# Layer pair on one core: residuals laid into PSUM by ScalarE, sums added by DMAs, and the seven-product form from group 4

## The chip, the core and the metric

The kernel runs on one core of a Trainium2 chip. The engines of the core work side by side, each on its own queue of instructions: TensorE (PE in the profile, its weight loads PEld), VectorE (DVE), ScalarE (ACT), GpSimd (POOL) and SyncE (SP), which issues most DMAs. The metric is the device time of one execution in microseconds (us), lower is better; times are medians over runs.

## The reference

The input is 2 images of 56 x 56 tokens with 384 channels in float32. Layer 0 is a neighbourhood attention with an MLP, layer 1 a mixer with an MLP:

```python
# layer 0
h = neighborhood_attention(layer_norm(x, ln1_g, ln1_b), w_qkv, ...)   # 12 heads, 7 x 7 window
x = x + h
y = layer_norm(x, ln2_g, ln2_b)
x = x + (gelu(y @ w1 + b1) @ w2 + b2)                                  # 384 -> 1536 -> 384
# layer 1
h = layernorm(x, n1_g, n1_b)
p = h @ w_in + b_in                                                    # 384 -> 768
local = depthwise_conv_3x3(p, k_conv)
lr, rl = ema_scan(local, axis=2), ema_scan(local, axis=2, reverse=True)  # along a line
tb, bt = ema_scan(local, axis=1), ema_scan(local, axis=1, reverse=True)  # along a column
mixed = 0.25 * (lr + rl + tb + bt) + local                             # y[i] = 0.6 y[i-1] + 0.4 x[i]
mixed = layernorm(mixed, on_g, on_b)
x = x + (mixed @ w_out + b_out)
h2 = layernorm(x, n2_g, n2_b)
x = x + (gelu(h2 @ w1 + b1) @ w2 + b2)
```

The change touches the MLP of layer 0 and all of layer 1; the attention stays as it is.

## The kernel before

The 6272 tokens are 49 tiles of 128. After the attention, the rest of the kernel (`passes`) goes over them twice, in groups of 4 tiles (512 tokens).

The *first pass* (loop at L1712, groups 0 to 12, of which group 0 has one tile) computes the MLP of layer 0 for group g and `project_in` (L1472, the product with `w_in`) for group g-1. `hidden` (L1190) makes one of twelve 128-channel slices of the hidden layer: three matmuls of 512 columns and a GELU on ScalarE. `tokens` (L1198) multiplies the hidden layer by `w2` for one tile of 128 tokens, twelve matmuls of 384 columns into one of two PSUM banks, `y` and `y_end`, which `bank()` gives out in turn. L1846 then adds the residual `x` on VectorE and writes `x2`, and `norm.add` takes the statistics of that row. `store_x2` writes `x2` to DRAM.

In groups 1 and 2 (`EARLY`), in the hidden layer of group 3, and in the tail below, products take a *seven-product form* (`hidden_by_seven` L1538, `tokens_by_seven` L1620): two-by-two blocks are multiplied with seven products instead of eight, from sums of weights (`sums_of_w1` L1509, `sums_of_w2` L1601), of the input (`sums_of_input` L1523) and of the hidden layer, which GpSimd makes.

The convolution and the scans of layer 1 are VectorE work that runs *beside* TensorE, in a pool opened by `begin_convolution` (L1713). `Band` (L1237) handles some lines of one image for one of six 128-channel slices (`BANDS`: four bands for image 0, three for image 1). It loads `pt` from DRAM, ScalarE takes the centre tap (`centre`), VectorE the other eight taps (L1281), `loc` is stored; then both scan directions along the lines (`both_ways` L1225, in parts of at most `LINES` = 20 lines) give `both`, L1297 forms `both*share + loc`, and this goes to `mix_d` in DRAM. `Columns` (L1306) does the scans along columns of one slice of one image: `turn` transposes the lines (GpSimd for the first job of an image, else ScalarE, L1328), `both_ways` scans in quarters of 14 lines, L1355 adds `share` times that to `mixed`, loaded from `mix_d`, and the sum is stored back.

`Beside` (L112) sets where this work stands in the program's order. It holds a list of jobs; each job is a generator that issues an instruction or two and yields its estimated us (`us`, L1221). After each piece of TensorE work the program calls `beside.go(worth)`: worth times `rate` is added to a balance, and jobs are stepped until it is used up. `MLP, PRO, ROW = 2.25, 2.5, 6.2` are the worths of a hidden slice, a `project_in` slice and a token row in the first pass, `MLP_D, OUT_D, ROW_D` those of the second stage; the rate is 0.9 and becomes 1.0 once image 1 is reached. `until(name)` issues all that is left up to a job, and `later` puts off a store by a step.

The *second stage* (loop at L1885, groups 0 to 5) takes the MLP of layer 1 for group g and `project_out` (L1434) for group g+1: twelve matmuls with `w_out` a row, `xc = ps*rs + x` on VectorE (L1440), and the statistics of that. The statistics of `mixed` come from `measure_beside` (L1423), which has TensorE turn `mx` into a PSUM tile (`xi`). `load_mix` (L1373) loads `mx` and `x`. For the group where both images meet, `half_way` = 6, it first issues all that is left of the convolution.

The *tail* (loop at L1926) does groups 6 to 11 in the seven-product form, with the statistics turned by VectorE (`measure_by_vector` L1405) and the transposes by VectorE (`turned` L1162); group 12 has one tile. Its pool and the weight sums come at the start of group 5 of the second stage (L1886).

Rows of biases (`b2_0`, `b_out`, `b2_1`) are added by `add_row` (L1122) to whole groups of 4 tiles ahead of their use as residuals. `Norm` (L205) holds a group's statistics: `close` takes the root on GpSimd, `shift` (VectorE) the product of mean and root, `apply_by_scalar` normalises on ScalarE.

Of the kernel before, what the change touches and what calls it, by code (L numbers as in the profile page):

```python
# [33 lines left out]
F32 = mybir.dt.float32  # L34
# [29 lines left out]
    ((0, 19), (19, 37), (37, 47), (47, 56)),  # L64
    ((0, 18), (18, 36), (36, 56)),
)
HALF = H // 2
LINES = 20
# [46 lines left out]
class Beside:  # L115
# [3 lines left out]
    def __init__(self):  # L119
        self.jobs, self.due, self.finished, self.idle = [], 0.0, set(), True  # L120
        self.late, self.rate = [], 0.9
        self.steps = self.run()
# [8 lines left out]
    def later(self, issue):  # L131

        self.late.append([1, issue])

    def step(self):
        got = next(self.steps)
        for entry in self.late:
            entry[0] -= 1
        while self.late and (self.late[0][0] < 0 or got is None):
            self.late.pop(0)[1]()  # L140
        return got
# [17 lines left out]
    def go(self, worth):  # L159
        self.due += self.rate * worth  # L160
# [15 lines left out]
def block_kernel(ctx: ExitStack, tc: tile.TileContext, ins: dict, out: bass.AP):  # L176
# [25 lines left out]

# [3 lines left out]
    class Norm:  # L206
# [15 lines left out]
        def close(self, k, n=P, first=0):  # L222
# [4 lines left out]
            nc.gpsimd.tensor_tensor(rs, rs, mhalf[:n, first:k], ALU.pow)  # L227

# [853 lines left out]
    def passes(xs, xn, w1, w2, between=lambda ps: None):  # L1082
# [9 lines left out]
        half_way = next(g for g, (t, n) in enumerate(dgroups) if t + n * P > T1)  # L1092
# [29 lines left out]
        def add_row(x, n, name):  # L1122

            engine = nc.vector if beside.busy() else nc.gpsimd
            engine.tensor_tensor(
                x[:, :n, :], x[:, :n, :], row(name).unsqueeze(1).to_broadcast([P, n, C]), ALU.add
            )

        def prepare_w_out():
# [11 lines left out]
            t = flat(half("sums", "out", 3))  # L1141
            nc.vector.tensor_copy(t[:2, 2 * C : 3 * C], ps[:2, :])
# [56 lines left out]
        def tokens(lhs, w, k, ps=None):  # L1199

            ps = bank() if ps is None else ps
            for m, t in enumerate(lhs):
                nc.tensor.matmul(  # L1203
                    ps, lhsT=t[:, k * P : (k + 1) * P], rhs=w[:, m, :],
                    start=m == 0, stop=m == len(lhs) - 1,
                )
            return ps

# [28 lines left out]
        class Band:  # L1237
# [21 lines left out]
            def centre(self):  # L1259
                if self.loc is None:  # L1260
                    self.loc = half("loc", "work")
# [6 lines left out]
            def steps(self):  # L1268
# [5 lines left out]
                for dy in (-1, 0, 1):  # L1274
# [13 lines left out]
                beside.later(lambda: nc.sync.dma_start(  # L1288
                    out=loc_d[self.b][self.m, :, at], in_=flat(loc)))
                both = half("both", "out", 3)[:, : self.n]  # L1290
                parts = -(-self.n // LINES)
                for i in range(parts):
                    part = slice(self.n * i // parts, self.n * (i + 1) // parts)
                    yield from both_ways(both[:, part], loc[:, part])
                    if i == 0:
                        behind = beside.behind()
                nc.vector.scalar_tensor_tensor(  # L1297
                    flat(both), flat(both), share, flat(loc), ALU.mult, ALU.add
                )
                if isinstance(behind, Band):  # L1300
                    behind.centre()
                yield us(self.n)
                beside.later(lambda: nc.sync.dma_start(
                    out=mix_d[self.b][self.m, :, at], in_=flat(both)))

        class Columns:  # L1306
# [16 lines left out]
            def turn(self, copy):  # L1323
                c, t = len(self.lines), half("line", "work")
# [9 lines left out]
            def steps(self):  # L1334
# [5 lines left out]
                for c in range(2):  # L1340
                    t = self.lines[c]
                    for i in range(0, HALF, QUARTER):
                        yield from both_ways(t[:, i : i + QUARTER], t[:, i : i + QUARTER])
                        if c == 0 and i == 0:
                            self.turn(nc.scalar.copy)
                            for h in range(2):
                                mixed.append(half("mixed", "out", 3))
                                nc.sync.dma_start(out=flat(mixed[h]), in_=self.rows(mix_d, h))
                    if c == 1:
                        behind = beside.behind()  # L1350
                    for i in range(0, HALF, QUARTER):
                        at = slice(c * HALF + i, c * HALF + i + QUARTER)
                        for h in range(2):
                            to = mixed[h][:, :, at]
# [707 lines left out]
```

## Time and profile before

| | us |
|---|---|
| median of 3 runs (lowest, highest) | 2594.55 (2593.26, 2600.41) |
| the profiled execution, its own time | 2598.4 |
| its span | 2596.6 |

The span runs from the first to the last instruction of the profile; 1.8 us lie around it. The profile gives busy time by engine over the span, the span in 40 slices of 64.9 us, groups of instructions by line and tile (busy us, mean ns of one, then the engine's idle time ahead of them and what released it), and a timeline by engine. A line number is that of the kernel before. The matmuls' ends are modelled, so starts are the safer marks.

DMA work, of which the change moves some to another queue, stands so in the page:

```profile
DMA packets 131652, 299.17 MB, mean 115 GB/s; under 512 B 10390, under 2 KB 85760, under 8 KB 129152
## 3 DMA queue, kind: packets, MB, share of 16 engines
q1 hardware_dynamic: 126512, 269.76, 30.2%
q10 hardware_dynamic: 4944, 26.74, 3.0%
```

All DMAs of before are issued by SyncE and ScalarE.

### The profile page before, as it was taken

What the parts mean: (1) busy time and instruction counts of PE and PEld (TensorE: products, weight loads), DVE (VectorE), ACT (ScalarE), POOL (GpSimd) and SP (SyncE); (2) the same over time, 40 slices, a digit from 0 to 9 for tenths busy, and PEclk for the clock granted to TensorE, in tenths of its full rate; (3) what the DMA queues carried; (4) which work ended last, traced back from release to release, by engine and by line L of the source; (5) the groups of instructions that cost most, each with busy time, mean ns of one, the idle gap of its engine ahead of it and who ended that gap; (6) DMA issues with size and microseconds to landing.
All of it is one profiled execution on the core that took longest, in us unless ns stands there. A gap on an engine that the chain in (4) does not pass through costs nothing. (4 is left out here: it accounts for less than half of the span.)

```text
span 2596.6 us, 39994 instructions
## 1 busy us (share of the span) xinstructions
PE 2570.7 (99%) x16146; PEld 1644.1 (63%) x16148; DVE 1964.2 (76%) x3481; ACT 982.9 (38%) x1748; POOL 467.0 (18%) x457
## 2 busy tenths in 40 slices
PE   9999999999999999999999999999999999999999
PEld 5666666666798644555555555555555557888888
DVE  4888878887444288688998889889988836888871
ACT  5656555654443332322344423212233312333222
POOL 0111211121552100000010000000010042344432
PEclk9999999999999999999999999999999999999999
DMA  7423454225311132332346534533354321111000
GB/s 230 154 85 98 155 191 141 86 93 192 114 34 37 59 128 84 109 115 100 127 153 237 199 120 168 180 124 122 105 213 172 136 101 46 49 49 49 22 13 18
DMA packets 131652, 299.17 MB, mean 115 GB/s; under 512 B 10390, under 2 KB 85760, under 8 KB 129152
## 3 DMA queue, kind: packets, MB, share of 16 engines
q1 hardware_dynamic: 126512, 269.76, 30.2%
q10 hardware_dynamic: 4944, 26.74, 3.0%
q8 instruction: 129, 2.11, 0.3%
q14 instruction: 67, 0.55, 0.1%
HBM read 180.86 MB, written 115.61 MB: 114 GB/s over the span
## 5 line engine op out<-in xcount | busy, mean ns | idle before, releaser
L1185 PE MATMUL mm<-hT,w 128*128 128x512 f32 x1080 | 473.6, 593 | 0.1
L1281 DVE SCALAR_TENSOR_TENSOR loc<-pt,taps,loc 128x990 f32<-128x990 f32 (+9 forms) x336 | 377.2, 1123 | 10.2 <-ACT loc L1263 1.9
L1185 PEld LDWEIGHTS mm<-hT,w 128*128 128x128 f32 x1080 | 201.8, 190 | 239.0 <-issue 231.4
L227 POOL TENSOR_TENSOR rs<-rs,mhalf 128x4 f32<-128x4 f32 (+4 forms) x72 | 89.3, 1240 | 1269.9 <-DVE rs L224 1261.3
L1196 ACT ACTIVATE hid<-mm,chan 128x512 f32<-128x512 f32 x180 | 123.3, 686 | 405.9 <-PE mm L1185 405.8
L1203 PE MATMUL y<-w,hid 128*128 128x384 f32 x792 | 260.9, 486 | 0.0
L1203 PE MATMUL y_end<-w,hid 128*128 128x384 f32 x792 | 260.8, 486 | 0.0
L551 DVE TENSOR_TENSOR pts<-sc,bias 119x448 f32<-119x448 f32 (+5 forms) x396 | 219.3, 617 | 45.4 <-PE sc L540 45.1
L561 ACT ACTIVATE pts<-pts 119x448 f32<-119x448 f32 (+5 forms) x396 | 210.9, 573 | 112.1 <-DVE pts L551 107.2
L1203 PEld LDWEIGHTS y_end<-w,hid 128*128 128x128 f32 x792 | 149.9, 190 | 102.8
L1203 PEld LDWEIGHTS y<-w,hid 128*128 128x128 f32 x792 | 149.8, 190 | 102.8 <-issue 0.5
L394 PE MATMUL ps<-hT,wqkv 128*128 128x448 f32 x504 | 204.8, 550 | 2.1 <-ACT vs L439 1.5
L1185 PE MATMUL mm<-hT,w_in 128*128 128x512 f32 x396 | 172.0, 593 | 1.5 <-DVE hid_u L1571 0.9
L394 PEld LDWEIGHTS ps<-hT,wqkv 128*128 128x128 f32 x504 | 91.3, 189 | 84.4 <-issue 74.2
L1185 PEld LDWEIGHTS mm<-hT,w_in 128*128 128x128 f32 x396 | 75.0, 190 | 96.2 <-issue 91.9
L1168 DVE STREAM_TRANSPOSE hT<-xn 32x96 f32<-32x96 f32 x464 | 125.0, 269 | 11.6 <-ACT xn L245 5.6
L245 ACT ACTIVATE xn<-xc,sh,rs 128x384 f32<-128x384 f32 x98 | 64.4, 699 | 170.2 <-DVE sh L238 170.1
L1414 DVE STREAM_TRANSPOSE turned<-mx 32x192 f32<-32x192 f32 x336 | 124.0, 369 | 4.4
L580 PE MATMUL o<-pts,vt 100*32 100x112 f32 (+3 forms) x3168 | 117.0, 265 | 1.8 <-ACT pts L561 1.8
L540 PEld LDWEIGHTS sc<-qT,kT 32*100 32x100 f32 (+3 forms) x3168 | 87.8, 169 | 46.9 <-DVE sum L570 7.6
L540 PE MATMUL sc<-qT,kT 32*100 32x112 f32 (+3 forms) x3168 | 106.5, 268 | 3.5 <-DVE pts L551 3.5
L610 PE MATMUL ps<-wproj,og 128*128 128x384 f32 x294 | 106.4, 501 | 2.8 <-DVE og L523 2.1
(179 smaller groups left out, 4144.4 us busy)
## 6 DMA issues: line engine op xcount, KB each, us to landing
loc<-loc_d SPq DMA_DIRECT2D x24, 784.0 KB
mixed<-mix_d SPq DMA_DIRECT2D x24, 784.0 KB
mix_d<-mixed SPq DMA_DIRECT2D x24, 784.0 KB
xa<-x_d SPq DMA_DIRECT2D x24, 768.0 KB
bias<-in_bias_t ACTq DMA_DIRECT2D x13, 1344.0 KB
p_d<-mx SPq DMA_DIRECT2D x11, 1536.0 KB
mx<-mix_d SPq DMA_DIRECT2D x11, 1536.0 KB
pt<-p_d SPq DMA_DIRECT2D x18, 560.0 KB
```

The costliest lines, as they stand in the source:

```text
L394: nc.tensor.matmul(ps, lhsT=wqkv[:, c, m * P : (m + 1) * P], rhs=hT[:, c, half_of(n)], start=c == 0, stop=c == NC - 1,)
L540: nc.tensor.matmul(sc[i // 2][: w.keys, i % 2, q : q + TT], lhsT=kT[d, hg, w.keys_at + r * w.kc : w.keys_at + (r + w.rows) * w.kc], rhs=qT ...
L551: nc.vector.tensor_tensor(self.pts[:n, h : h + 2, lo:hi, :], sc[half][:n, :, at * TT : (at + hi - lo) * TT].rearrange("p h (c q) -> p h c ...
L561: nc.scalar.activation(t, t, AF.Exp)
L580: nc.tensor.matmul(o[i * HD : (i + 1) * HD, self.slot, :TT], lhsT=w.vt[:n, c, h * HD : (h + 1) * HD], rhs=self.pts[:n, i, c, :], start=c = ...
L610: nc.tensor.matmul(ps, lhsT=ogs[t // 7][:, c, at : at + P], rhs=wproj[:, c, :], start=c == 0, stop=c == NC - 1,)
L1168: nc.vector.transpose(hT[j : j + HD, :, k * P + i : k * P + i + HD], xn[i : i + HD, k, :].rearrange("p (c q) -> p c q", c=NC)[:, :, j : j ...
L1185: nc.tensor.matmul(ps[:, : n * P], lhsT=w[:, c, m * P : (m + 1) * P], rhs=hT[:, c, : n * P], start=c == 0, stop=c == NC - 1,)
L1196: nc.scalar.activation(t[:, : n * P], ps[:, : n * P], AF.Gelu, bias=col(b1, m))
L1203: nc.tensor.matmul(ps, lhsT=t[:, k * P : (k + 1) * P], rhs=w[:, m, :], start=m == 0, stop=m == len(lhs) - 1,)
L1281: nc.vector.scalar_tensor_tensor(to, pt[:, lo + dy - self.top : hi + dy - self.top, xt : xt + n], self.tap(dy, dx), to, ALU.mult, ALU.add,)
L1414: nc.vector.transpose(t[j : j + HD].rearrange("p (m c) -> p m c", m=NI)[:, :, i : i + HD], mx[i : i + HD, :, k * P + j : k * P + j + HD],)
```

## The change

- **Seven-product form from group 4 on** (`switch = 4` in place of `half_way` = 6). The second stage's loop does groups 0 to 3; after `project_out` of group 4 it issues all that is left of the convolution, closes its pool, and makes the weight sums; `load_mix` no longer waits.
- **Residual in the bank.** In groups 3 to 12 of the first pass, ScalarE copies the residual row into the bank (`seeded`), `tokens` accumulates onto it (no first flag), and ScalarE copies the result out to `x2`. Each bank is written once by a matmul of zeros beforehand (`primed`). Statistics of row k-1 follow the matmuls of row k, those of the last row the first hidden slice of the next group. `close_by_pool` takes the product of mean and root on GpSimd.
- **Row scans.** `loc` is stored twice, to `loc_d` and `mix_d`; `both` is multiplied by `share` on ScalarE eight steps later, and GpSimd issues a DMA that adds it to `mix_d` eleven steps later.
- **Bias rows.** `add_row` issues an accumulating DMA on GpSimd's queue in place of an addition on VectorE or GpSimd; `b_out` is added in the second stage for all groups.
- **Bands and columns.** Five bands for image 0 and four for image 1; row scans of a whole band; column scans of 28 lines; mixing in halves of 28. `decay` is as long, and is filled by GpSimd in the convolution's pool. One more buffer each for `work` and `out` tiles.
- **Order.** Constants of `Beside` are 2.6, 3.9 and 7.8, rate 1.0 and then 0.93, less the statistics' own time. The groups of the first pass without convolution work no longer turn their transposes on VectorE.

```diff
-    ((0, 19), (19, 37), (37, 47), (47, 56)),
-    ((0, 18), (18, 36), (36, 56)),
+    ((0, 19), (19, 28), (28, 37), (37, 47), (47, 56)),
+    ((0, 18), (18, 36), (36, 45), (45, 56)),
...
-    def go(self, worth):
-        self.due += self.rate * worth
+    def go(self, worth, own=0.0):
+        self.due += self.rate * worth - own
...
+        def close_by_pool(self, k):
+            self.sh = self.small.tile([P, NT], F32, name="sh")
+            off = self.small.tile([P, NT], F32, name="off")
+            rs = self.rs[:, :k]
+            nc.vector.tensor_scalar(rs, self.mv[:, :k, 1], EPS, 1.0, ALU.add, ALU.mult)
+            nc.vector.tensor_scalar_mul(off[:, :k], self.mv[:, :k, 0], -1.0)
+            nc.gpsimd.tensor_tensor(rs, rs, mhalf[:, :k], ALU.pow)
+            nc.gpsimd.tensor_tensor(self.sh[:, :k], off[:, :k], rs, ALU.mult)
...
-        half_way = next(g for g, (t, n) in enumerate(dgroups) if t + n * P > T1)
+        switch = 4
...
-            engine = nc.vector if beside.busy() else nc.gpsimd
-            engine.tensor_tensor(
-                x[:, :n, :], x[:, :n, :], row(name).unsqueeze(1).to_broadcast([P, n, C]), ALU.add
+            nc.gpsimd.dma_start(
+                out=x[:, :n, :], in_=row(name).unsqueeze(1).to_broadcast([P, n, C]),
+                accum_op=ALU.add,
             )
...
-        def tokens(lhs, w, k, ps=None):
+        def tokens(lhs, w, k, ps=None, onto=None):
-            ps = bank() if ps is None else ps
+            ps = onto if onto is not None else bank() if ps is None else ps
             for m, t in enumerate(lhs):
                 nc.tensor.matmul(
                     ps, lhsT=t[:, k * P : (k + 1) * P], rhs=w[:, m, :],
-                    start=m == 0, stop=m == len(lhs) - 1,
+                    start=m == 0 and onto is None, stop=m == len(lhs) - 1,
+                    skip_group_check=onto is not None,
                 )
...
+        def seeded(x, k):
+            ps = bank()
+            nc.scalar.copy(ps, x[:, k, :])
+            return ps
+        def primed(t):
+            nc.tensor.matmul(t, lhsT=zeros[:, :P], rhs=zeros[:, : t.shape[1]], start=True, stop=True)
...
-                beside.later(lambda: nc.sync.dma_start(
-                    out=loc_d[self.b][self.m, :, at], in_=flat(loc)))
-                both = half("both", "out", 3)[:, : self.n]
...
-                nc.vector.scalar_tensor_tensor(
-                    flat(both), flat(both), share, flat(loc), ALU.mult, ALU.add
-                )
+                for to in (loc_d, mix_d):
+                    beside.later(lambda to=to: nc.sync.dma_start(
+                        out=to[self.b][self.m, :, at], in_=flat(loc)))
+                both = half("both", "out", 4)[:, : self.n]
+                yield from both_ways(both, loc)
...
-                yield us(self.n)
-                beside.later(lambda: nc.sync.dma_start(
-                    out=mix_d[self.b][self.m, :, at], in_=flat(both)))
+                beside.later(lambda: nc.scalar.mul(flat(both), flat(both), share), 8)
+                beside.later(lambda: add_to_mix(self.b, self.m, at, both), 11)
+
+        def add_to_mix(b, m, at, src):
+            nc.gpsimd.dma_start(out=mix_d[b][m, :, at], in_=flat(src), accum_op=ALU.add)
...
-        MLP, PRO, ROW = 2.25, 2.5, 6.2
-        MLP_D, OUT_D, ROW_D = 2.15, 2.5, 7.0
+        MLP, OUT, ROW = 2.6, 3.9, 7.8
+        STATS = 0.75
...
-            for k in () if early else range(n):
+            for k in range(n) if g == 0 else ():
                 ps = tokens(hid, w2, k)
                 nc.vector.tensor_tensor(x2[:, k, :], ps, x[:, k, :], ALU.add)
                 norm.add(k, [x2[:, k, :]])
-                if g < last or k < n - 1:
-                    beside.go(ROW)
+            for k in range(n) if g >= EARLY.stop else ():
+                ps = tokens(hid, w2, k, onto=seeds.pop(0))
+                if k:
+                    norm.add(k - 1, [x2[:, k - 1, :]])
+                beside.go(ROW, STATS if k else 0.0)
+                nc.scalar.copy(x2[:, k, :], ps)
+                if k + 2 < n:
+                    seeds.append(seeded(x, k + 2))
...
-        for g, (t0, n) in enumerate(dgroups[:half_way]):
-            if g == half_way - 1:
-
+        beside.rate = 0.93
+        for g, (t0, n) in enumerate(dgroups[:switch]):
+            hid = []
+            for m in range(NHID):
+                hid.append(hidden(w1, m, hT, n, "L1_conv_b1"))
+                beside.go(MLP, measure_beside(m, g + 1, ahead))
+            res = x3
+            x3, norm = project_out(g + 1, *ahead)
+            ahead = load_mix(g + 2)
+            if g == switch - 1:
+                beside.until((1, NI - 1))
                 cctx.close()
...
-            if g < half_way:
+            if g < switch:
                 continue
...
+            add_row(ahead[1], n_next, "b_out")
```

## The prediction

> **What bounds the kernel now.** I read the page's busy totals and slices first, then busy times of chosen stretches, then TensorE's timeline, and only then the groups of the other engines.
>
> ```profile
> PE 2570.7 (99%) x16146; PEld 1644.1 (63%) x16148; DVE 1964.2 (76%) x3481; ACT 982.9 (38%) x1748; POOL 467.0 (18%) x457
> PE   9999999999999999999999999999999999999999
> DVE  4888878887444288688998889889988836888871
> PEclk9999999999999999999999999999999999999999
> ```
>
> TensorE (PE) is full in every slice at full clock; VectorE (DVE) is far from full as a mean, but at 8 or 9 tenths in the middle. The next answer shows one period of each of three stages, with the busy time of PE, PEld, DVE, ACT, POOL: a group of the first pass, an ordinary group of the second stage, a seven-product group.
>
> ```profile
> 1232.00:1312.00 80.00, 80.00 (x230) 41.34 (x229) 73.17 (x109) 25.64 (x39) 3.26 (x2) 1.00 0.33 113
> 1831.00:1912.00 81.00, 81.00 (x253) 44.59 (x252) 71.03 (x73) 18.51 (x25) 8.04 (x6) 1.00 0.41 143
> 2229.00:2301.00 72.00, 71.68 (x351) 61.53 (x350) 60.37 (x166) 21.60 (x45) 29.52 (x26) 1.00 0.13 44
> ```
>
> So in all three, time goes only if matmuls go; work taken from another engine is worth nothing by itself. TensorE's timeline (start, us) gives the periods and the only late row in the second stage:
>
> ```profile
> 1072.32 28.49 PE L1185 MATMUL mm<-hT,w 128*128 128x512 f32 x66
> 1152.25 28.49 PE L1185 MATMUL mm<-hT,w 128*128 128x512 f32 x66
> ...
> 1830.94 10.46 PE L1185 MATMUL mm<-hT,w 128*128 128x512 f32 x24
> 1912.23 10.46 PE L1185 MATMUL mm<-hT,w 128*128 128x512 f32 x24
> ...
> 1961.24 7.90 PE L1203 MATMUL y<-w,hid 128*128 128x384 f32 x24
> ...
> 2117.26 4.14 PE L1203 MATMUL y<-w_out,mx 128*128 128x384 f32 x12 [1.03 <-DVE xc L1440]
> 2183.18 4.03 PE L1203 MATMUL y<-w_out,mx 128*128 128x384 f32 x12
> 2255.04 4.03 PE L1203 MATMUL y<-w_out,mx 128*128 128x384 f32 x12
> ```
>
> First-pass group: 1152.25 - 1072.32 = 79.93. Ordinary second-stage group: 1912.23 - 1830.94 = 81.29. Seven-product group: 2255.04 - 2183.18 = 71.86.
>
> **What the Trainium skill says.** "DMA: Bandwidth & Descriptors", section "SWDGE vs HWDGE vs iDMA": a DMA that accumulates can only be issued from GpSimd, whose cores write its descriptors. Its section "Anatomy of one DMA" fits 2.0 us + bytes/436e3 to such a transfer. The trace before has no GpSimd DMA, so nothing here agrees or disagrees. "SBUF — State Buffer", section "Who interferes with whom": a VectorE instruction with two SBUF inputs and a GpSimd one that reads SBUF exclude each other. The trace agrees (a scan of 2.47 us beside a GpSimd copy, shown below, against a mean of 1.81). "PSUM — Partial Sum Buffer", section "The four PSUM rules": a matmul without the first flag adds only where an earlier matmul has set the element's bit. That is why the two banks are primed; no run shows it yet.
>
> **The change, part by part.** The rows used, from the groups kept apart by shape (busy us, mean ns, then idle time and its releaser):
>
> ```profile
> L1846 DVE TENSOR_TENSOR xc<-y,xa 128x384 f32<-128x384 f32 x21 | 11.7, 558 | 84.4 <-PE y L1203 84.2
> L1297 DVE SCALAR_TENSOR_TENSOR both<-both,loc 128x1008 f32<-128x1008 f32 x18 | 21.6, 1202 | 0.4
> L1228 DVE TENSOR_TENSOR_SCAN line<-decay,line 128x784 f32<-128x784 f32 x48 | 86.6, 1805 | 7.0 <-POOL line L1328 3.9 <-ACT line L1328 3.0
> L1125 POOL TENSOR_TENSOR xa<-xa,rows 128x1536 f32<-128x1536 f32 x10 | 34.4, 3440 | 54.7 <-DMA xa<-x_d 44.3 <-ACT xn L245 10.4
> L439 ACT COPY vs<-ps 128x384 f32<-128x384 f32 x49 | 22.8, 476 | 41.4 <-PE ps L432 29.1 <-DMA v_d<-vs 11.7 <-ACT pts L561 0.3
> ```
>
> **1. Seven products from group 4 (was 6).** Groups 4 and 5 change form: 2 x (81.29 - 71.86) = 18.86 us of PE. In one group: four token rows 30.97 to 27.30, 24 measuring transposes (2.6) and 12 channel transposes (1.3) handed to DVE, hidden layer about 1.9. PE had no gap there, so all of it counts: **-18.9**. Before, at 2117, GpSimd's nine weight sums (5 x 1.81 + 4 x 2.62 = 19.5) stood ahead of a normalisation that DVE and then PE waited for: 1.03. They now come after project_out of group 4, with no normalisation of that group behind them: **-1.0**.
>
> **2. Residual in the bank.** In groups 3 to 12, 40 rows: DVE loses 40 x 0.558 = 22.3 us. ACT gains 40 copies into and 40 out of the bank, at 0.48 (the row above) to 0.57 (a 512-wide copy): about 41 us. At 25.6 of 80 busy it has room. PE gets a new wait: row k+2 starts only when ACT has copied row k out and laid the residual in, about 1.1 us of work in the 7.74 us of row k+1. That leaves 6.6 us for what stands ahead in ACT's queue: a centre tap (1.13) or the turn of a column pair (4 x 0.93 = 3.7, seldom two such). Cost 0; without that cover, each row pays its excess. The two priming matmuls (0.33 each) fall into a 0.87 us gap that PE has at 859: 0.
>
> **3. Row scans added by DMA.** DVE loses L1297: 21.6 plus 23.9 in its other shapes = 45.5 us. ACT gains 54 multiplications, about 47 us; GpSimd's queue 54 accumulating DMAs of 252 to 532 KB, estimate 3.2 us each by the fit. A pending descriptor delays only later GpSimd work, and GpSimd is busy 3 of 80 us here. Columns read the sum later, behind the taps of later bands. Bounds: 0, and 3 us once should the last band's sum reach the first column late. I take 0.
>
> **4. Bias rows by DMA.** 39 DMAs (37 of 768 KB, estimate 3.8 us) replace L1125: DVE loses 31 us, GpSimd 62. Each is issued at least half a group before its reader: 0 on PE.
>
> **5. Bands and columns.** 54 jobs instead of 42: more instructions for the same pixels. The taps row (377.2 over 336) plus some 21 us, row scans plus 4.5. Columns scan 28 lines at once: 3.4 us against 2 x 1.8, about -12; mixing 784 wide 1.51 against 2 x 0.87, about -5.
>
> **6. VectorE in sum.** -22.3 - 45.5 - 31 + 25.5 - 17 = -90. It had 1001 busy of 1168 us from 907 to 2075, and its convolution work must now end some 105 us earlier, at the end of project_out(4) (1961 on the old clock). 1001 - 90 - 13 (group 4's own) = 898 of about 1072 us, 84%: it fits, against 86% before. The pace is now set in PE's own times (2.6, 3.9, 7.8), rate 1.0: about 78 of 79.9 us per first-pass group are handed out as estimated, but row scans and taps run 2 to 3% and columns 8% below these estimates. The second stage, at 0.93, hands out 72.6 of 81.3.
>
> **7. The switch.** A flush of the convolution stands after project_out(4), call its PE end P. By the orders of both kernels, left in front of row 0's addition on DVE are three column scans (3.4 each), four mixings (1.5), small ones and one row's statistics (1.4): the addition ends about P + 18.8. PE needs that bank for row 2 at P + 15.5: **+3.4**. GpSimd's weight sums wait for nothing but PE until the fourth, which takes the convolution's space and so waits for the last scan at P + 15; then input sums end about P + 34, wanted at P + 37: 0. If the space is free only when the stores of the result land, these slip by some 7 us (a load of two such tiles issued at 1326.26 landed about 1333.3): rival C.
>
> **8. Column start in the first pass.** GpSimd turns the first column job:
>
> ```profile
> 1332.02 0.91 POOL L1328 COPY line<-loc 128x392 f32<-128x392 f32 x1
> 1333.28 4.12 POOL L1328 COPY line<-loc 128x392 f32<-128x392 f32 x3 [0.35 <-DMA loc<-loc_d]
> 1334.22 2.47 DVE L1228 TENSOR_TENSOR_SCAN line<-decay,line 128x784 f32<-128x784 f32 x1 [1.27 <-POOL line L1328]
> ```
>
> Now the scan spans 28 lines and waits for all four copies, not two, after the 7 us of its load: a hole of about 8.5 us in DVE. It delays that group's normalisation; bounds 0 (room as before) and 4; I take **+2**, once.
>
> Sum: -18.9 - 1.0 + 3.4 + 2 = **-14.5**. The profiled execution of before took 2598.4 (span 2596.6 and 1.8 around it), so such a one would take 2583.9. It lies 3.85 above the median, 2594.55; taken from the median the forecast is **2580**.
>
> **Rivals.** **A**, the sum above. **B, slower: ACT's hand-over of banks.** Every row now needs an ACT turnaround where DVE's addition was before. The place is the four token rows of ten groups; the price what ACT's queue holds beyond 6.6 us: with a centre, a multiplication held back by a late scan and a turn pair in the same row, 1.5 us twice a group is 10 x 3 = 30, so 2610. It decides once the loss passes 22.3 us in all (2.2 per group): then the result is over 0.3% slower. For it: multiplications and turns wait in order on DVE, whose pace is now tight. Against it: ACT's 26 of 80 us and a full row of slack. **C: late at the switch.** Left-over DVE work, or sums waiting for stores, cost 8 us beyond A's: 2588. For it: nothing else covers PE there; against: DVE's 84%. **D: no new stalls.** Parts 7 and 8 cost nothing: 2594.55 - 19.9 = 2574.7. For it: the work runs below its handed-out estimates. That the change doesn't do what it says is no rival: instruction counts of the changed program show two more seven-product groups.
>
> **How the numbers follow.** A 0.55, D 0.16, C 0.17, B 0.12. A measurement can tell about 0.3% (7.8 us) from no change, so faster means under 2586.8, slower over 2602.3. A and D are faster (0.71), and two fifths of C (0.06); the rest of C is within; B gives 0.10 slower, and 0.02 within for its milder end: faster 0.77, same 0.13, slower 0.10. A's own range is 2575 to 2587. The range for 8 in 10 starts at 2573 (D and one us of other gaps) and reaches 2593, over C's centre with its store bound; B is left out.
>
> **What would show it.** Three first-pass periods near 79.9 with no wait on ACT ahead of the token rows (else B); eight seven-product groups at 71.9 instead of six; row 2 after project_out(4) waiting 3 us for DVE's addition (none: D; PE's first input-sum matmul waiting on GpSimd: C); the first column group a few us long; DVE's total near 1895. The forecast is wrong if a stall repeats per group, since each us per group is 10 us, or if accumulating DMAs take tens of us and hold GpSimd's queue ahead of a normalisation.

## The result, and the profile after

| | before | after |
|---|---|---|
| median of 12 runs, us | 2597.57 | 2597.04 |
| ratio, with its 95% interval | | 0.9998 (0.9985 to 1.0012) |
| the profiled execution (span), us | 2598.4 (2596.6) | 2597.85 (2596.0) |

No difference. The forecast was 2580, a ratio of 0.994; its median of before came from three runs and lay 3.0 us below that of twelve. The page of after, busy totals and two of the slice rows:

```profile
PE 2556.8 (98%) x16342; PEld 1679.8 (65%) x16342; DVE 1961.2 (76%) x3660; ACT 1076.8 (41%) x1943; POOL 565.4 (22%) x593
...
PE   9999999999999999999999999999998999999999
...
DVE  4888878887344389967799979878886778878871
```

TensorE's busy time fell by 13.9 us (some 4.6 us of slow matmuls, shown below, are still in it), and yet the span stayed: TensorE now waits, and one slice shows an 8. What it waits for, from the convolution's start to the end, first in before and then in after (total us, times, longest; two smaller ones of after left out):

```profile
PE uz L1552 <- POOL xsums L1533: 1.3, 4, 0.3
PE y L1203 <- DVE xc L1440: 1.0, 1, 1.0
PE mm L1185 <- ACT hT L262: 0.6, 1, 0.6
```

```profile
PE y L1213 <- DVE xc L1922: 10.8, 1, 10.8
PE mm L1195 <- ACT hT L272: 5.3, 1, 5.3
PE mm L1195 <- ACT hid L1206: 0.8, 1, 0.8
PE mm L1195 <- ACT mx L1476: 0.8, 1, 0.8
```

Two waits carry nearly all of it. TensorE's timeline of after, with group starts and these waits:

```profile
1311.10 18.19 PE L1195 MATMUL mm<-hT,w 128*128 128x512 f32 x42
1330.08 10.57 PE L1195 MATMUL mm<-hT,w 128*128 128x512 f32 x24 [0.79 <-ACT hid L1206]
...
1353.04 7.99 PE L1195 MATMUL mm<-hT,w_in 128*128 128x512 f32 x18 [0.79 <-ACT mx L1476]
...
1393.14 28.49 PE L1195 MATMUL mm<-hT,w 128*128 128x512 f32 x66
...
1674.49 13.07 PE L1195 MATMUL mm<-hT,w 128*128 128x512 f32 x24 [5.30 <-ACT hT L272]
...
1920.94 10.46 PE L1195 MATMUL mm<-hT,w 128*128 128x512 f32 x24
...
1996.39 9.99 PE L1213 MATMUL y<-w,hid 128*128 128x384 f32 x24 [10.79 <-DVE xc L1922]
```

After each of the long waits the matmuls themselves are slow as well: 24 of 512 columns took 13.07 us where 10.57 stood in the same place before, 24 of 384 columns 9.99 instead of 7.90. Busy times by stretch show it as a lower granted clock (the figure after the five engines'): 0.97 in the group behind the first wait, 1.00 in the group after that, 0.95 in the group of the switch:

```profile
1675.00:1758.00 83.00, 83.00 (x251) 45.09 (x250) 60.57 (x91) 21.34 (x33) 10.78 (x11) 0.97 0.60 151
1758.00:1840.00 82.00, 82.00 (x255) 45.12 (x254) 64.90 (x79) 26.75 (x37) 12.32 (x12) 1.00 0.64 178
1921.00:2015.00 94.00, 83.21 (x253) 45.42 (x252) 67.50 (x56) 25.75 (x35) 36.97 (x17) 0.95 0.45 158
```

Stretch by stretch, from starts on the two timelines (us):

| stretch | before | after | change | forecast |
|---|---|---|---|---|
| groups 4 and 5, and the seven-product form's start, to the first project_out row within group 6 | 189.67 | 168.88 | -20.8 | -19.9 |
| group 3 of the second stage (the switch) | 81.28 | 94.33 | +13.05 | +3.4 |
| first project_out to the second stage's first slice, and its group 0 | 115.50 | 123.17 | +7.7 | 0 |
| group 9 of the first pass (before: the one with the first column job) | 79.94 | 82.04 | +2.1 | +2 |
| all else from the pass's start on | | | +0.1 | 0 |

The sum is +2.15; the attention before it, which the change doesn't touch, happened to end 2.73 earlier, hence the span 0.6 shorter. In the last row, the stretch ahead of the convolution takes 1.7 more (189.82 after 188.11), the last group 0.8, and the rest 2.4 less; most of this is in the later seven-product groups, 71.40 us each instead of 71.86, where the short waits on GpSimd's input sums are gone. No run shows why.

**The wait at the switch.** VectorE's timeline there, and one row of GpSimd's beside it:

```profile
1977.98 4.98 DVE L1248 TENSOR_TENSOR_SCAN line<-decay,line 128x1568 f32<-128x1568 f32 x1
1982.99 1.65 DVE L1250 SCALAR_TENSOR_TENSOR line<-line 128x28 f32<-128x28 f32 x1
1984.67 4.94 DVE L1252 TENSOR_TENSOR_SCAN line<-decay,line 128x1568 f32<-128x1568 f32 x1
1989.64 4.59 DVE L1369 SCALAR_TENSOR_TENSOR mixed<-line,mixed 128x784 f32<-128x784 f32 x2
1994.16 1.71 DVE L248 SCALAR_TENSOR_TENSOR sh<-mv,rs 128x4 f32<-128x4 f32 x1
1995.79 0.55 DVE L1922 TENSOR_TENSOR xc<-y,xc 128x384 f32<-128x384 f32 x1
```

```profile
1979.76 4.81 POOL L1515 TENSOR_TENSOR w_t<-w,w_t 128x768 f32<-128x768 f32 x1
```

The instructions in front of row 0's addition are the ones that the forecast counted, but beside GpSimd's weight sums each takes longer: scans 4.98 and 4.94 (3.4 otherwise), the small one 1.65 (0.21), two mixings 4.59 (3.14 just before), `sh` 1.71 (0.17): 7.5 us in all. The extra is nearly the same each time, 1.4 to 1.6 us, whether the instruction takes 3.4 us or 0.17: close to one of GpSimd's sums (1.81), as if the two engines took turns. GpSimd's sum suffers too, 4.81 against 1.81.

**The wait at the second stage's start.** ScalarE's timeline, then SyncE's queue of DMA issues (time, then what the issue took):

```profile
1673.05 0.71 ACT L1283 ACTIVATE loc<-pt,taps 128x504 f32<-128x504 f32 x1 [4.45 <-DMA pt<-p_d]
1673.67 2.10 ACT L272 ACTIVATE hT<-tp,chan 128x512 f32<-128x512 f32 x3
```

```profile
1649.13 0.95 SPq L1392 DMA_DIRECT2D mx<-mix_d  x1
1650.13 0.80 SPq L648 DMA_DIRECT2D xa<-x_d  x1
1651.04 5.96 SPq L664 DMA_DIRECT2D w<-in_L_conv_w  x3
...
1660.98 0.43 SPq L1270 DMA_DIRECT2D pt<-p_d  x1
```

A band's tile, 308 KB, is issued at 1660.98 behind 4.6 MB of other loads and is there at 1673.0, 12 us later. Its centre tap stands in ScalarE's queue ahead of the channel copies that TensorE needs, so TensorE waits for a transfer that has nothing to do with it.

### The profile page after: what moved, and what is told of

Its sections match the earlier page's. It is cut to its first block, busy times and chain, and to the rows that moved or that the text cites. A ratio compares the mean times of both kernels' runs of the same rounds, so it can differ in the third digit from the quotient of the medians.

```text
span 2596.0 us, 41217 instructions
## 1 busy us (share of the span) xinstructions
PE 2556.8 (98%) x16342; PEld 1679.8 (65%) x16342; DVE 1961.2 (76%) x3660; ACT 1076.8 (41%) x1943; POOL 565.4 (22%) x593
## 5 line engine op out<-in xcount | busy, mean ns | idle before, releaser
L1301 DVE SCALAR_TENSOR_TENSOR loc<-pt,taps,loc 128x495 f32<-128x495 f32 (+13 forms) x432 | 398.2, 922 | 118.5 <-ACT loc L1283 105.0
L1195 PE MATMUL mm<-hT,w 128*128 128x512 f32 x936 | 413.1, 596 | 6.1 <-ACT hT L272 5.3
L1195 PEld LDWEIGHTS mm<-hT,w 128*128 128x128 f32 x936 | 175.8, 191 | 216.2 <-issue 201.5
L1213 PE MATMUL y<-w,hid 128*128 128x384 f32 x696 | 231.4, 490 | 10.8 <-DVE xc L1922 10.8
L1213 PE MATMUL y_end<-w,hid 128*128 128x384 f32 x696 | 229.2, 486 | 0.0
L1213 PEld LDWEIGHTS y_end<-w,hid 128*128 128x128 f32 x696 | 131.8, 190 | 90.6
L1178 DVE STREAM_TRANSPOSE hT<-xn 32x96 f32<-32x96 f32 x592 | 159.6, 270 | 23.2 <-ACT xn L255 15.5
L1417 DVE STREAM_TRANSPOSE turned<-mx 32x192 f32<-32x192 f32 x464 | 171.2, 369 | 6.1
L227 POOL TENSOR_TENSOR rs<-rs,mhalf 128x4 f32<-128x4 f32 (+4 forms) x55 | 60.0, 1091 | 372.1 <-DVE rs L224 362.3
L1320 POOL DMA_DIRECT2D mix_d<-both x54 | 50.9, 942 | 365.5 <-ACT both L1316 324.3
```

The source lines that it names most:

```text
L1178: nc.vector.transpose(hT[j : j + HD, :, k * P + i : k * P + i + HD], xn[i : i + HD, k, :].rearrange("p (c q) -> p c q", c=NC)[:, :, j : j ...
L1195: nc.tensor.matmul(ps[:, : n * P], lhsT=w[:, c, m * P : (m + 1) * P], rhs=hT[:, c, : n * P], start=c == 0, stop=c == NC - 1,)
L1213: nc.tensor.matmul(ps, lhsT=t[:, k * P : (k + 1) * P], rhs=w[:, m, :], start=m == 0 and onto is None, stop=m == len(lhs) - 1, skip_group_c ...
L1301: nc.vector.scalar_tensor_tensor(to, pt[:, lo + dy - self.top : hi + dy - self.top, xt : xt + n], self.tap(dy, dx), to, ALU.mult, ALU.add,)
L1417: nc.vector.transpose(t[j : j + HD].rearrange("p (m c) -> p m c", m=NI)[:, :, i : i + HD], mx[i : i + HD, :, k * P + j : k * P + j + HD],)
```

## The experiments

Each starts from the changed kernel unless it says otherwise; "before" was run beside each. Ratios are to before.

| run | median us | ratio (95% interval) |
|---|---|---|
| pace 1.0 in the second stage | 2593.01 | 0.9975 (0.9964 to 0.9986) |
| w2 loads later | 2592.65 | 0.9985 (0.9977 to 0.9993) |
| weight sums held back | 2592.36 | 0.9982 (0.9970 to 0.9994) |
| switch at 6 | 2606.98 | 1.0033 (1.0021 to 1.0045) |
| both cures | 2578.30 | 0.9923 (0.9911 to 0.9935) |
| both cures, turn split | 2575.09 | 0.9918 (0.9905 to 0.9931) |
| residual additions back on VectorE | 2607.08 | 1.0039 (1.0026 to 1.0051) |
| row scans' sum back on VectorE | 2614.11 | 1.0056 (1.0042 to 1.0071) |
| bias rows back on the engines | 2595.33 | 0.9990 (0.9980 to 1.0001) |
| both cures, turn split, early bias rows back | 2576.34 | 0.9919 (0.9903 to 0.9936) |

### What holds the bank at the switch

```diff
-        beside.rate = 0.93
+        beside.rate = 1.0
```

> The changed kernel with the second stage's pace at 1.0 instead of 0.93, so that no scan or mixing is left in front of row 0's addition when the convolution is flushed at the switch. Theory A (left-over VectorE work, lengthened by GpSimd's weight sums beside it, holds the bank): the wait of 10.8 us before row 2 and the slow restart of about 2.1 us both go, the group falls from 94.3 to about 81.4 us, and the time to about 2584 (ratio to before 0.995). Rival B (the nine weight sums and the closing of the convolution's space hold the first seven-product group, whatever is left on VectorE): the wait moves to the input sums, the stretch from group 3's hidden layer to the first seven-product matmul stays above 90 us, and the time stays near 2597. Rival C (VectorE is late in the second stage at this pace): new waits on project_out's additions in each of four groups, 1 us or more each.

The group of the switch took 81.29 us instead of 94.33, without a wait: the left-over work was the cause, and neither the nine sums nor the closing of the space held anything. But at the higher pace image 1's first scan of columns came 40.4 us after its group's start instead of 51.1, in the project_out that group 1 does for group 2:

```profile
1802.32 3.42 DVE L1248 TENSOR_TENSOR_SCAN line<-decay,line 128x1568 f32<-128x1568 f32 x1 [6.36 <-POOL line L1344]
...
1805.96 0.62 DVE L1446 SCALAR_TENSOR_TENSOR xc<-y,rs,xa 128x384 f32<-128x384 f32 x1
```

VectorE stood idle 6.36 us for a column that GpSimd was turning, with project_out's ready addition queued behind the scan; TensorE waited 3.2 us and that group took 87.57 instead of 81.28. So 13.0 were won and 6.3 given back, once and not per group; the median fell by 4.0 us, to 2593.01 and not to 2584. The second-stage start cost 6.0 us of waiting here.

```diff
-                w1_sums = sums_of_w1(w1, three)
-                w2_sums, steps = sums_of_w2(w2)
-                for step in steps:
-                    step()
...
                 nc.vector.tensor_tensor(o, ps, o, ALU.add)
+                if g == switch - 1 and k == 0:
+                    seen = sm.tile([P, NT], F32, name="seen")
+                    nc.gpsimd.tensor_copy(seen, o[:, :NT])
+                    w1_sums = sums_of_w1(w1, three)
+                    w2_sums, steps = sums_of_w2(w2)
+                    for step in steps:
+                        step()
```

> The changed kernel with GpSimd's nine weight sums at the switch held back until row 0's addition is done, so that they don't run beside the last scans. Theory A (GpSimd's reads and VectorE's two-input instructions exclude each other): scans there take 3.4 us instead of 4.95, a pair of mixings 3.1 instead of 4.6, and the wait before row 2 falls from 10.8 to about 3.4 us; the sums then end late, and the first input sum costs a wait of 2 to 6 us; in all 1 to 5 us less than the changed kernel. Rival B (the scans are long for another reason, DMA traffic or the long tile): they stay near 5 us, the wait before row 2 stays near 10.8, and the late sums add 8 us or more, about 2605.

VectorE's timeline of this run, then TensorE's two waits:

```profile
1979.79 3.43 DVE L1248 TENSOR_TENSOR_SCAN line<-decay,line 128x1568 f32<-128x1568 f32 x1
1983.50 3.42 DVE L1252 TENSOR_TENSOR_SCAN line<-decay,line 128x1568 f32<-128x1568 f32 x1
1986.96 3.12 DVE L1369 SCALAR_TENSOR_TENSOR mixed<-line,mixed 128x784 f32<-128x784 f32 x2
```

```profile
1990.67 8.01 PE L1213 MATMUL y<-w,hid 128*128 128x384 f32 x24 [3.25 <-DVE xc L1918]
...
2012.33 1.71 PE L1547 MATMUL uz<-xsums,w_t 128*128 128x256 f32 x4 [3.14 <-POOL xsums L1528]
```

With the same VectorE instructions in the same order and GpSimd silent, scans take 3.4 again and the wait is 3.25, against the 3.4 of the forecast. The sums, now late, cost 3.14. Overlap with GpSimd, and nothing in the scans themselves, made the difference of 7.5 us.

### What makes the second stage start late

```diff
-        for part in w_parts[3:]:
-            part()
         project_in(g, hT, first_input)
+        for part in w_parts[3:]:
+            part()
```

> The changed kernel with the three 768 KB loads of the second MLP's w2 issued after project_in of the last group instead of ahead of it. Theory A (a band's tile queued behind these loads lands after 12 us, the centre tap that waits for it stands ahead of the channel copies in ScalarE's queue, and TensorE waits 5.3 us and restarts slowly): that tile lands within 8 us, the wait before the second stage's first hidden slice falls below 1 us, the time to about 2589 (7.7 less). Rival B (the accumulating DMAs fill the DMA engines there, not the weights): the tile is as late as before and the wait stays within 2 us of 5.3.

ScalarE's timeline of this run:

```profile
1666.45 0.70 ACT L1283 ACTIVATE loc<-pt,taps 128x504 f32<-128x504 f32 x1
1667.06 2.10 ACT L272 ACTIVATE hT<-tp,chan 128x512 f32<-128x512 f32 x3
```

The tile, issued at 1658.89, was there before the centre tap came up at 1666.45: under 7.6 us. TensorE's wait fell to 0.7, the stretch and the group behind it from 123.17 to 116.1, by 7.1. The span came out at 2586.3; by the medians the gain is less, 2592.65, ratio 0.9985.

```diff
-            nc.gpsimd.dma_start(
-                out=x[:, :n, :], in_=row(name).unsqueeze(1).to_broadcast([P, n, C]),
-                accum_op=ALU.add,
+            engine = nc.vector if beside.busy() else nc.gpsimd
+            engine.tensor_tensor(
+                x[:, :n, :], x[:, :n, :], row(name).unsqueeze(1).to_broadcast([P, n, C]), ALU.add
             )
```

> The changed kernel with the bias rows added by VectorE while convolution work is there and by GpSimd otherwise, as before. Theory A (these DMAs bring nothing to TensorE by themselves; their 25 MB are part of the crowd on the DMA engines at the start of the second stage): the stretch from the last project_out of the first pass to the second stage's first hidden slice falls from 39.3 towards 34.1 us, the stretch ahead of the convolution from 189.8 to 188.1, and VectorE's 1.75 us a group cost under 3 us in all; the wait at the switch stays 10.8: total 2590 to 2598. Rival B (as with the additions put back: work put back on VectorE at a pace of 1.0 makes first-pass groups wait): one or more first-pass groups grow by 2 us or more, total above 2600.

ScalarE's timeline of this run:

```profile
1674.71 0.71 ACT L1283 ACTIVATE loc<-pt,taps 128x504 f32<-128x504 f32 x1 [1.89 <-DMA pt<-p_d]
```

The wait there fell to 2.7 us and the stretch with its group from 123.17 to 118.1. That the bias rows' DMAs are part of the crowd is not shown by this: the tile, issued at 1665.11, took 9.6 us, but in the run with the residual additions back (below), which keeps these DMAs, it took 9.8 (issued at 1672.39, used at 1682.23) and TensorE waited 2.8 us. What the two runs share is a last group of the first pass that is about 1.9 us longer. In the other runs that keep all these DMAs the tile took 10.6 to 13.8 us. Here the last group took 84.08 instead of 82.20, with VectorE's statistics late; the stretch ahead of the convolution stayed at 189.76. In sum 2595.33, inside the first theory's span, but with one period close to what the second had, and without the gain ahead of the convolution that the first had.

### What the parts of the change are worth

```diff
-        switch = 4
+        switch = 6
...
+            if g == switch - 2:
+                beside.until((1, NI - 1))
             ahead = load_mix(g + 2)
             if g == switch - 1:
-
-                beside.until((1, NI - 1))
```

> The changed kernel with the seven-product form from group 6 on as before, everything else of the change kept (the flush stands ahead of the load for group 6). Theory A (the rest of the change is worth nothing on TensorE by itself and costs its own stalls at the first column job, 2.1 us, and at the start of the second stage, 7.7): 18.9 us for two groups in the old form, less 13.1 for the stall at the switch, so 5.8 over the changed kernel: about 2603, ratio to before 1.002 to 1.004. Rival B (freeing VectorE pays by itself): at or below 2597.

2606.98, some 4 us over the 2603 worked out; the second stage's start cost 7.0 us of waiting here, and the two groups 81.28 each. Without the earlier switch the rest of the change, taken together, is worth nothing: this run is slower than before, by 0.2 to 0.45%.

```diff
...
-                ps = tokens(hid, w2, k, onto=seeds.pop(0))
+                ps = tokens(hid, w2, k)
...
-                nc.scalar.copy(x2[:, k, :], ps)
-                if k + 2 < n:
-                    seeds.append(seeded(x, k + 2))
+                nc.vector.tensor_tensor(x2[:, k, :], ps, x[:, k, :], ALU.add)
```

> The changed kernel with the residual added on VectorE again in groups 3 to 12 (no copies into and out of the bank on ScalarE, first flag on the matmuls). Theory A (work taken from VectorE in the first pass is worth nothing on TensorE by itself, and ScalarE's hand-over costs nothing either): all periods of the first pass within 0.3 us of the changed kernel's, total within 2 us of it. Rival B (VectorE at a pace of 1.0 has no room for 2.2 us more a group): first-pass periods grow by 0.5 us or more each, 5 us or more in all. Rival C (the hand-over of banks costs): periods fall.

The first theory fell. Seven of the first pass's nine periods stayed within 0.2 us, but TensorE waited for VectorE's additions in two places:

```profile
1300.82 9.70 PE L1213 MATMUL y<-w,hid 128*128 128x384 f32 x24 [2.95 <-DVE xc L1852]
...
1650.64 4.14 PE L1213 MATMUL y_end<-w_out,mx 128*128 128x384 f32 x12 [2.36 <-DVE xc L1852]
```

The first is behind the first column job. VectorE's timeline of this run:

```profile
1282.97 3.42 DVE L1248 TENSOR_TENSOR_SCAN line<-decay,line 128x1568 f32<-128x1568 f32 x1 [12.14 <-POOL line L1344]
...
1296.90 3.42 DVE L1252 TENSOR_TENSOR_SCAN line<-decay,line 128x1568 f32<-128x1568 f32 x1
1300.24 0.53 DVE L1852 TENSOR_TENSOR xc<-y,xa 128x384 f32<-128x384 f32 x1
```

VectorE had waited 12.14 us for the first turned column, so all that was queued behind it came late, the addition that frees a bank among it. That group took 84.84 instead of 79.94, the last 84.03 instead of 82.20. The residual in the bank is thus not only fewer us on VectorE: it takes VectorE off the way by which TensorE gets its banks back. The waits on it don't repeat per row; none of them is on ScalarE's hand-over.

```diff
...
+                nc.vector.scalar_tensor_tensor(
+                    flat(both), flat(both), share, flat(loc), ALU.mult, ALU.add
+                )
...
-                beside.later(lambda: nc.scalar.mul(flat(both), flat(both), share), 8)
-                beside.later(lambda: add_to_mix(self.b, self.m, at, both), 11)
+                yield us(self.n)
+                beside.later(lambda: nc.sync.dma_start(
+                    out=mix_d[self.b][self.m, :, at], in_=flat(both)))
```

> The changed kernel with the row scans' sum formed on VectorE again and stored once (no multiplication on ScalarE, no accumulating DMA for it). Theory A (the 45 us taken from VectorE buy the early switch: by the handed-out order one more column scan pair with its mixings, about 10 us of VectorE work, then stands in front of row 0's addition): the wait before row 2 grows from 10.8 to about 21 us or more, beside GpSimd's sums, total about 2607. Rival B (VectorE has slack enough): the wait stays within 3 us of 10.8.

```profile
1836.52 13.62 PE L1195 MATMUL mm<-hT,w 128*128 128x512 f32 x24 [2.96 <-ACT hT L272]
...
2014.00 11.06 PE L1213 MATMUL y<-w,hid 128*128 128x384 f32 x24 [28.39 <-DVE xc L1925]
```

28.4 us, more than the 21 worked out: some of the 45 us was absorbed on the way, the rest stood at the switch. Another wait is new, 2.96 us: ScalarE's turn of a column, which waits for the load of `loc`, stands ahead of the channel copies; with the slow matmuls behind it this cost 6.3 us in two groups (84.41 and 84.43 instead of 81.28). The second stage's start had no wait (34.12 us for the stretch of 39.28), although its w2 loads stood where the changed kernel has them. This run leaves out the second store and the accumulating DMAs there, but it also has its convolution work at another point: the tile whose centre tap precedes the channel copies was issued at 1645.36, ahead of the other loads. Which of the two took the wait away is open.

### Both cures, and one more

```diff
         for g, (t0, n) in enumerate(dgroups[:switch]):
+            if g == 2:
+                beside.rate = 1.05
...
-        for part in w_parts[3:]:
-            part()
         project_in(g, hT, first_input)
+        for part in w_parts[3:]:
+            part()
```

> The changed kernel with both cures: the w2 loads after project_in of the last group, and the second stage's pace raised from 0.93 to 1.05 from its group 2 on, so that the first column job of image 1 stands where it stood and nothing of the convolution is left in front of row 0's addition at the switch. Theory A (the two stalls are all that stands between the forecast and the result): the wait before the second stage's first hidden slice under 1 us, the wait before row 2 under 1 us, no new wait; 7.7 + 13.1 = 20.8 us less than the changed kernel, about 2576, ratio to before 0.992. Rival B (a wait removed comes back elsewhere, as at the first column job of image 1 with pace 1.0 throughout): one new wait of 3 us or more, ratio 0.994 to 0.997.

The switch group took 81.56, the second stage's start with its group 116.1, and no new wait came: 2578.30, ratio 0.9923, where 2576 and 0.992 were expected. The forecast's gain is there once these two stalls are out.

```diff
-                        if c == 0 and step == 0:
+                        if c == 0 and step == 1:
                             self.turn(nc.scalar.copy)
+                        if c == 0 and step == 0:
                             for h in range(2):
```

> As the run with both cures, and the second half of a column job's turn (four of the eight copies that stand one behind another on ScalarE, 6.7 us) one step later, so that GELUs come in between. Theory A (the 2.1 us that the first column job of image 0 costs is ScalarE's block of copies ahead of the GELUs and of project_in's bias, with three banks of cover): the two waits of 0.8 us there go and the group falls from 82.05 to about 80 us, the total by about 2 us against the run with both cures. Rival B (as the prediction had it: a hole in VectorE, which waits for its first column, delays a normalisation): the group stays at 82.

ScalarE's timeline in group 9, and then all that TensorE waits for from the convolution's start on:

```profile
1320.31 3.38 ACT L1344 COPY line<-loc 128x392 f32<-128x392 f32 x4
1324.20 0.68 ACT L1206 ACTIVATE hid<-mm,chan 128x512 f32<-128x512 f32 x1
1324.77 3.39 ACT L1344 COPY line<-loc 128x392 f32<-128x392 f32 x4
```

```profile
PE mm L1195 <- ACT hT L272: 0.7, 1, 0.7
PE tp L269 <- DVE st L219: 0.4, 1, 0.4
```

Group 9 fell from 82.07 to 79.93: its 2.1 us were ScalarE's eight copies in a row, not VectorE's hole. At 2575.09, ratio 0.9918, this is ahead of both kernels; its lead over the run with both cures alone is within the spread of the runs.

```diff
+            if name == "b2_0" and not beside.busy():
+                nc.gpsimd.tensor_tensor(
+                    x[:, :n, :], x[:, :n, :], row(name).unsqueeze(1).to_broadcast([P, n, C]), ALU.add
+                )
+                return
```

This one is on top of the last version.

> The run with both cures and the split turn, and in the groups ahead of the convolution GpSimd adds the bias row again in place of the DMA. Theory A (there the extra DMA traffic makes the next group's tile later, VectorE's statistics of it stand ahead of an addition that TensorE waits for): the stretch from the first matmul of the pass to the convolution's start falls from 189.65 to about 188.1 us, the total by 1.5 us. Rival B (the later statistics have another cause): it stays within 0.4 us of 189.65.

189.79, as long as with the DMAs. Why the groups ahead of the convolution take 1.7 us more than before stays open; TensorE waits there for two additions of `hid_u`, one of them behind statistics of a tile for which VectorE waits 3.55 us instead of 2.90.

## Why the prediction was wrong

By the stretches the change came to +2.15 us where -14.5 was forecast. Of these 16.6 us, one step makes 9.6 and a second 7.7.

- **Part 1** held: 20.8 us for 19.9.
- **Part 7 is the first step that failed**, by its size: +3.4 became +13.05. The mechanism, the place, and the instructions in front of row 0's addition were as forecast. Two terms were missing in the sum. The left-over scans and mixings were priced at their mean although GpSimd's weight sums were counted for the same microseconds, and the prediction itself had quoted a scan of 2.47 us against 1.81 beside a GpSimd copy, and what the Trainium skill says in "SBUF — State Buffer", section "Who interferes with whom": that a VectorE instruction with two SBUF inputs and a GpSimd one that reads SBUF exclude each other. The trace agrees (4.98 us for a scan of 3.4). This is 7.5 us, shown by holding the sums back. And a wait was counted as its own length: the matmuls behind it took 2.1 us more.
- **The second is a stall that no part had**, 7.7 us at the second stage's start. Parts 3 to 5 costed the new DMAs and the bands by what they take from each engine and gave 0 for TensorE, since each DMA is issued early enough for its own reader. Part 3's words for it, that a pending descriptor "delays only later GpSimd work", left out what they do to another transfer and to the instruction that waits for it. By the traces, 10.0 MB moved in the 38 us from 1637 on where before moved 6.7 MB in the 31 us up to the same point of the program. That the tile's lateness behind the w2 loads makes this stall is shown: with these loads later 7.1 us of it went, and the stretch with its group took 116.1 us in the runs with both cures as well. But before had the same loads there and no such stall, so the change brought the other part of the cause, and what that is stays open: the bias rows' DMAs (out: 5.1 us less), the second store with the added sums (out: 7.7 less), or the other places that VectorE's work and the bands then have. None of the runs separates these. The bands of nine lines leave less time for the next load to land; that part was not tried by itself.
- **Rival B** had the right engine, ScalarE's queue in order, and the wrong place: it looked at the token rows, where the hand-over never cost anything in any run, and not at the other readers of that queue. **Rival C** had the right place and, by luck, nearly the size: 8 us beyond the sum's 3.4, where 9.6 were measured. But it priced more left-over work or sums waiting for stores. The left-over work was as much as the sum had counted, made slower by the overlap, and no late store held TensorE. **Rival D**'s ratio, 0.992, is what the changed kernel reaches with its two stalls out.
- **Part 8** had the right size (+2, measured 2.1) by luck, for the wrong reason. The hole in VectorE is there, 10.2 us in front of the first column scan at 1278.12, but its group, the one before group 9, took 79.94 as ever: with the residual in the bank no addition waits behind it. In group 9 TensorE waited for a GELU and for a bias copy of project_in behind eight copies in a row on ScalarE, 6.7 us, of which part 2 had counted four, "seldom two such".
- **Part 6** held as a share, VectorE busy 890 us of the 1064 from 905.8 to the end of the project_out ahead of the switch, 84% as worked out; but a share says nothing of what is left in front of one addition. Its sign, a total near 1895, did not come: it was 1961.2, since the transposes of two more seven-product groups put 82 us on VectorE, in a stage where it has room.
- **Part 2**, "cost 0", was right for the token rows, but the opening's "work taken from another engine is worth nothing by itself" was too strong: with the additions back on VectorE the changed kernel is 10 us slower, though before, at its slower pace, TensorE did not wait for them. The run without part 3's 45 us off VectorE waits 17.6 us more at the switch.

## What to carry to other kernels

When work is moved in front of a flush, price it at what it takes beside whatever else starts there, and allow for slow matmuls behind the wait (1.7 to 3.2 us here, though not behind every one). For each new transfer ask whose load it delays, and then what else stands in the in-order queue behind the instruction that waits for that load. Work on an engine with slack is free until one of its instructions hands back a buffer that the bounding engine needs.

## What was not expected of the hardware

Behind most waits of about 3 us and more TensorE's matmuls took 1.7 to 3.2 us of extra time: after 5.30 (13.07 for 10.57), 10.79 (9.99 for 7.90), 28.39 (11.06 for 7.90), 3.23 (6.93 for 4.03), 2.95 (9.70 for 7.90) and 2.81 (12.26 for 10.57), but not behind the 3.25 us wait of the run with the sums held back (8.01 for 7.90), nor behind the 2.74 of the run with the bias rows back (10.57). The clock record of the changed kernel's trace shows where the time goes: the granted clock was 0.50 from 1672.7 to 1679.6 us and from 1990.2 to 2000.4, spells that began about 4 us after TensorE had stopped. It worked through 5.1 and 4.0 us of them, and half of that, 2.5 and 2.0, is the extra time (2.50 and 2.09 measured). Behind the waits of 3.25 and 2.74 us there is no such spell, and no run here shows what decides it.

Accumulating DMAs took longer than the prediction estimated from the fit that it took from the Trainium skill, which is for transfers issued from GpSimd in general: 252 KB landed in 4.5 us at the median, 504 KB in 7.1 and 532 KB in 5.5 (3.2 estimated), 768 KB in 7.2 and 7.8 (3.8 estimated), and 12 in the crowd at the second stage's start; each also held GpSimd for 0.9 to 1.4 us.
